# Local transformer: the softmax of the window attention by whole banks of 512 columns

## The chip, the cores and the metric

The program runs on one core of one Trainium2 chip. The metric is the device time of the program in microseconds (us); lower is better. The engines are TensorE (PE; its weight loads are PEld), VectorE (DVE), ScalarE (ACT), GpSimd (POOL) and SyncE (SP), which issues the DMAs.

## The reference, cut to what matters

The program computes two layers of a network on 16 sequences of 256 tokens and 128 features. Its longest part is the local transformer of the first layer: six blocks, each an attention over windows of 32 tokens (16 heads of 64) and a gated FFN. A window's queries see the keys of their own window and of the one before: 64 keys.

```python
q = l2norm(q) * qs
k = l2norm(k) * ksc
...
q = q * cos * scale + rotate_half(q) * sin * scale
k = k * cos * inv + rotate_half(k) * sin * inv
...
sim = jnp.einsum('bhwie,bhwje->bhwij', bq, bk2) * QK_SCALE
sim = jnp.where(mask, -jnp.finfo(sim.dtype).max, sim)
attn = jax.nn.softmax(sim, -1)
out = jnp.einsum('bhwij,bhwje->bhwie', attn, bv2)
```

The norms of `l2norm` are numbers per token and head. The kernel multiplies the inverse norm of a key into the key itself, and that of a query, `rn` (with the scale 8 in the tables), into the softmax.

## The kernel before, in words

The 16 sequences are taken in 8 units of two; a unit's state `z` is 128 features by 512 tokens and stays in SBUF. The local transformer is one loop over `n`, with 32 iterations to a block (8 units x 4), so 192 in all and some to drain. One iteration takes four heads through each stage of a pipeline, and every stage works for another iteration's heads: `n` is projected, `n - 1` rotated, `n - 3` has its key norms fetched, `n - 4` has its keys scaled, its scores and its softmax, `n - 5` has its probabilities transposed, then come the weighted sums (`n - 8`) and the merging into the block's output (`n - 9`). The loop stands under a manual schedule: on PE, DVE, ACT and POOL each engine runs its instructions in the order in which the code writes them. An FFN is a generator whose steps are taken in between (`go_on(behind)`).

Order of one iteration, with the lines of the profile:

1. `scaled` (L837, POOL): keys times their inverse norms, two operations. `merging` (L969, PE): 16 matmuls into the bank `y`.
2. In odd iterations `norms_rows(rk)`: PE transposes `rk` (L816), ACT copies it (L818), SP writes it to DRAM as `rkh`. `widened` (L828, SP) later reads it back into `kn`, spread over partitions.
3. `rotate` (L756, POOL): four additions of what a DMA (`got`) has moved across partitions.
4. `flipped` twice (L930, PE; copies at L938 on ACT and L936 on DVE): the probabilities `pr` are transposed; between the two, `windows` (L847) and `masked` (L863), which fills two score banks with the mask.
5. In even iterations `norms_sum` (L764, PE; L773, ACT). `weighted` (L948, PE; copies L963 on ACT, L961 on DVE).
6. `scores` (L885, PE): 64 small matmuls into the two banks, one for each parity of the heads. Each bank is 8 groups of 64 keys.
7. `maxima` (L897, L899, DVE): for each bank the largest score of each group, then `nb = -mx * rn`.
8. In even iterations `norms_inverse`: PE transposes the sums (L782), DVE clamps them and makes a first guess of the inverse root (L784, L793), POOL refines it in three Newton steps (L800 to L808), 13 small operations. The results are `rk` for the keys (used by step 2 of the next iteration) and `rq`, from which `rn` is cut.
9. `project` twice (L740, PE): query and key of two head pairs, four matmuls in all; ACT squares each bank (L743), DVE makes `sent` and `q` or `k` from it (L745, L748), SP sends `sent` to `got` (L750, L751). `exponentials` is a generator that `project` advances between its banks: 16 exponentials of 64 columns (L907, ACT), each with the bias and the scale of its group and with its sum read out of the accumulator.
10. `divided` (L920, DVE; L922, POOL): reciprocal of 8 sums and the scaling of half of `pr`, done for each half.

PSUM has eight banks: four general ones, used in turn (`mm`), three for scores (`sim`) and one for `y`. `pr` has one buffer.

Of the kernel before, what the change touches and what calls it, by code (L numbers as in the profile page):

```python
# [13 lines left out]
AF = mybir.ActivationFunctionType  # L14
ALU = mybir.AluOpType
# [29 lines left out]
def adaln_kernel(  # L45
# [33 lines left out]
    def small(tag, shape, bufs=4):  # L79
        return (stage.get("small") or sm).tile(list(shape), F32, tag=tag, name=tag, bufs=bufs)  # L80
# [561 lines left out]
    with ExitStack() as es:  # L642
# [133 lines left out]
        def norms_inverse(n2):  # L776


            pt = bank()
            for t in range(4):  # L780
                c = slice(t * 128, (t + 1) * 128)
                nc.tensor.transpose(pt[:, c], n2[:, c], ident)  # L782
            x = small("nx", (128, 4, 4, 4), 2)
            nc.vector.tensor_scalar(  # L784
                x,
                pt.rearrange("p (t g e) -> p t g e", t=4, g=4)[:, :, :, 0:4],
                1e-24,
                None,
                ALU.max,
            )  # L790
            x = x.rearrange("p t g e -> p (t g e)")
            y = small("ny", (128, 64), 2)
            nc.vector.tensor_scalar(  # L793
                y.bitcast(I32), x.bitcast(I32), -0.5, float(0x5F3759DF), ALU.mult, ALU.add
            )
            rk = small("rk", (128, 4, 8), 2)
            rq = small("rq", (128, 8, 4), 3)
            for it in range(3):
                a = small("na", (128, 64), 2)
                nc.gpsimd.tensor_tensor(a, x, y, ALU.mult)  # L800
                nc.gpsimd.tensor_tensor(a, a, y, ALU.mult)
                nc.gpsimd.tensor_scalar(a, a, -0.5, 1.5, ALU.mult, ALU.add)
                if it < 2:
                    nc.gpsimd.tensor_tensor(y, y, a, ALU.mult)
                else:
                    y, a = (v.rearrange("p (t j e) -> p t j e", t=4, j=2) for v in (y, a))
                    nc.gpsimd.tensor_tensor(rk, y[:, :, 0], a[:, :, 0], ALU.mult)
                    nc.gpsimd.tensor_tensor(  # L808
                        rq.rearrange("p e t -> p t e"), y[:, :, 1], a[:, :, 1], ALU.mult
                    )  # L810
            return rk, rq.rearrange("p (g h o) t -> p g h (o t)", g=2, h=2)

        def norms_rows(rk):

# [76 lines left out]
                                skip_group_check=True,  # L891
                            )

        def maxima(sim, rn):

            mx = small("mx", (128, 8))
            nc.vector.tensor_reduce(mx, sim.rearrange("p (b k) -> p b k", b=8), AX.X, ALU.max)  # L897
            nb = small("nb", (128, 8))
            nc.vector.scalar_tensor_tensor(nb, mx, -1.0, rn, ALU.mult, ALU.mult)  # L899
            return nb  # L900

        def exponentials(x, sims, nbs, rn, pr, ssum):

            for par in range(2):
                for st in range(4):
                    b = 4 * x + st
                    nc.scalar.activation(  # L907
                        pr[:, x, st, par, :],
                        sims[par][:, b * 64 : (b + 1) * 64],
                        AF.Exp,  # L910
                        bias=nbs[par][:, b : b + 1],
                        scale=rn[:, par, b : b + 1],
                        accum_out=ssum[:, x, st, par : par + 1],
                    )
                    if st % 2:
                        yield

        def divided(pr, ssum):
            rsum = small("rsum", (128, 8))
            nc.vector.reciprocal(rsum, ssum.rearrange("p t h -> p (t h)"))  # L920
            prf = pr.rearrange("p t h k -> p (t h) k")
            nc.gpsimd.tensor_tensor(  # L922
                prf, prf, rsum.unsqueeze(2).to_broadcast([128, 8, 64]), ALU.mult
            )

        def flipped(p, x, pr, prT):

            pt = bank()
            for st in range(4):
                nc.tensor.transpose(  # L930
                    pt[:, st * 128 : (st + 1) * 128],
                    pr[:, x, st].rearrange("p h k -> p (h k)"),
                    ident,
                )
            if x:
                nc.vector.tensor_copy(prT[:, p + x, :], pt)  # L936
            else:
                nc.scalar.copy(prT[:, p + x, :], pt)  # L938

        def weighted(j, xw, prT):  # L940

# [150 lines left out]
        while n < N + 9 or behind:  # L1092
            layer, at_ = divmod(n, per)
            if at_ == 13 and 0 < layer < DEPTH:
                wffs[layer] = load_ffn(layer)
            if 0 <= n - 4 < N:
                for m in (2 * (n - 4), 2 * (n - 4) + 1):
                    scaled(m, kns.pop(m))

            w, j = divmod(n - 9, QS)  # L1100
            if 0 <= w < DEPTH * NU:
                if j == 0:
                    pys[w] = psy.tile([128, 512], F32, tag="y", name="y")
                merging(j, zxs.pop((w, j)), vos[w // NU], pys[w])
                if j == QS - 1:
                    add_to_state(w % NU, pys.pop(w))
            if n % 2 and 3 <= n <= N + 1:
                home = norms_rows(rk)
            go_on(behind)
            go_on(merges)  # L1110
            if 0 <= n - 1 < N:
                for m in (2 * (n - 1), 2 * (n - 1) + 1):
                    rotate(m, qs[m], got.pop(m))
            if 0 <= n - 5 < N:
                i, u, p = place(n - 5)
                if p == 0:
                    prTs[i, u] = atile("prT", (128, NP, 512))
                flipped(p, 0, prs[n - 5], prTs[i, u])
            for s, lag in ((0, 7), (1, 9)):
                v, r = divmod(n - lag, QS)  # L1120
                if r == 0 and 0 <= v < DEPTH * NU:
                    xws[v, s] = windows(v % NU, s)
            sims = masked() if 0 <= n - 4 < N else None
            if 0 <= n - 5 < N:
                flipped(p, 1, prs.pop(n - 5), prTs[i, u])

            if n % 2 == 0 and 2 <= n <= N:
                n2 = norms_sum([squares.pop(m) for m in range(2 * n - 4, 2 * n)])
            v, r = divmod(n - 8, QS)
            if 0 <= v < DEPTH * NU:  # L1130
                zxs[v, r] = weighted(r, xws[v, r // 2], prTs[v // NU, v % NU])
            go_on(behind)
            if sims:
                m = 2 * (n - 4)
                rn = inverses[m // 4][:, m % 4 // 2]
                scores(sims, m, [qs.pop(m), qs.pop(m + 1)])
                pr = atile("pr", (128, 2, 4, 2, 64), 1)
                nbs = [maxima(sims[par], rn[:, par]) for par in range(2)]
                ssum = small("ssum", (128, 2, 4, 2))

            if n % 2 == 0 and 2 <= n <= N:
                rk, inverses[n // 2 - 1] = norms_inverse(n2)
            if 0 <= w < DEPTH * NU and j == QS - 1:
                behind.append(ffn(w % NU, w // NU))
            go_on(behind)
            between = exponentials(0, sims, nbs, rn, pr, ssum) if sims else iter(())
            for m in (2 * n, 2 * n + 1):
                if n < N:
                    i, u, p = place(n)
                    qs[m], squares[m], got[m] = project(i, u, m, wqk[p + m % 2], between)  # L1150
                if m % 2 == 0:
                    go_on(behind)
            if sims:
                for x in range(2):
                    for _ in between:
                        pass
                    divided(pr[:, x], ssum[:, x])
                    between = exponentials(1, sims, nbs, rn, pr, ssum) if x == 0 else iter(())
                prs[n - 4] = pr
            if 0 <= n - 3 < N:  # L1160
                for m in (2 * (n - 3), 2 * (n - 3) + 1):
                    kns[m] = widened(m, home)
            if layer + 1 < DEPTH:
                if at_ == 18:
                    merges.append(merged(layer + 1))
                if at_ > per - QS:
                    p = 2 * (at_ - (per - QS) - 1)
                    wqk[p : p + 2] = [load_qk(layer + 1, p), load_qk(layer + 1, p + 1)]
            if at_ == 0 and 0 < layer < DEPTH:
                wqk[NP - 2 :] = [load_qk(layer, NP - 2), load_qk(layer, NP - 1)]  # L1170
            n += 1
# [375 lines left out]
```

## Time and profile before

| | us |
|---|---|
| median of 3 runs (4256.94 to 4262.21) | 4258.86 |
| the profiled execution, its own time | 4254.63 |
| its span | 4252.8 |

The busy shares over the span are PE 94%, PEld 61%, DVE 66%, ACT 67%, POOL 62%. The mean granted TensorE clock is 0.983 (1 is full speed). In the page's 40 slices the local transformer fills slices 3 to 33; PE shows 9 (90% or more) in nearly all of them, ACT 6 or 7, and the DMA engines about 4. One iteration takes some 17 us: `scores` starts first at 299.5 us and last at 3572.4.

How to read it: a group of instructions is named by line, engine, operation and tiles (out<-in), with its count; behind the first bar stand its busy time in us and the mean of one in ns, behind the second the idle time of the engine just before it and what ended most of that time. In a timeline a row has its start in us from the span's start, its length, engine, line, operation and tiles, and in brackets the idle time before it. A matmul on float32 operands appears as two records.

### The profile page before, as it was taken

The numbers are of one execution on the slowest core, as the hardware profiler recorded it, in microseconds if no ns is written. First come the engines' busy times: TensorE is split into PE (matmuls) and PEld (weight loads), VectorE is DVE, ScalarE is ACT, GpSimd is POOL, SyncE is SP. The second block draws the span as 40 slices with busy tenths as digits, with TensorE's granted clock in tenths as the row PEclk, the third lists the DMA queues.
The fourth block names the chain that finished last, engine by engine and source line by source line (L and its number), as shares of the span: only waits on it lengthen the run. The fifth ranks groups of instructions, "written<-read, shape, count | busy, mean of one in ns | idle before, by whom it ended". The sixth has DMA issues, their size and how long they took to land.

```text
span 4252.8 us, 118394 instructions
## 1 busy us (share of the span) xinstructions
PE 3979.4 (94%) x45491; PEld 2576.8 (61%) x45491; DVE 2826.8 (66%) x6003; ACT 2839.5 (67%) x9800; POOL 2619.5 (62%) x3326
## 2 busy tenths in 40 slices
PE   7867999999999999999999999999999998899998
PEld 4534666666666666666666666666666666454544
DVE  6746667777676777667676767776676765455554
ACT  4535666766767666666766666766667665578785
POOL 5446666676666776676766677666767673343432
PEclk9889999999999999999999999999999999999999
DMA  1334344444444444444444444444444441100000
GB/s 40 40 95 106 100 108 102 113 103 106 109 100 113 106 108 104 106 115 104 104 107 104 114 101 109 106 105 113 105 104 100 108 102 58 46 3 6 4 6 6
DMA packets 193548, 371.06 MB, mean 87 GB/s; under 512 B 42538, under 2 KB 83417, under 8 KB 192985
## 3 DMA queue, kind: packets, MB, share of 16 engines
q1 hardware_dynamic: 192984, 363.50, 34.2%
q8 instruction: 360, 5.90, 0.6%
q14 instruction: 204, 1.66, 0.1%
HBM read 127.92 MB, written 8.91 MB: 32 GB/s over the span
## 4 chain that ended last, share of the span: by engine, by line
PE 45%; DVE 23%; ACT 19%; issue 6%; POOL 5%; DMA 1%; SPq 0%; POOLq 0%; DVEq 0%; ACTq 0%
ACT pr L907 10%; PE mm L948 9%; PE sim L885 7%; DVE sent L745 6%; PE mm L764 4%; ACT sq L743 4%; PE mm L930 4%; POOL pr L922 4%; DVE k L748 3%; DVE q L748 3%; PE mm L740 3%; DVE mx L897 2%; PE mm L847 2%; PE mm L1334 2%; DVE nb L899 2%
## 5 line engine op out<-in xcount | busy, mean ns | idle before, releaser
L907 ACT ACTIVATE pr<-sim,nb,rq 128x64 f32<-128x64 f32 x3072 | 1229.5, 451 | 336.9 <-DVE nb L899 328.9
L922 POOL TENSOR_TENSOR pr<-pr,rsum 128x512 f32<-128x512 f32 x384 | 398.3, 1042 | 809.9 <-DVE rsum L920 769.4
L907 ACT ACTIVATION_READ_ACCUMULATOR pr<-sim,nb,rq 128x1 f32 x3072 | 773.9, 252 | 0.0
L969 PEld LDWEIGHTS y<-zx,wvo 128*128 128x128 f32 x6144 | 715.7, 192 | 91.5 <-issue 88.7
L969 PE MATMUL y<-zx,wvo 128*128 128x128 f32 x6144 | 717.5, 275 | 1.3 <-ACT zx L963 1.2
L740 PE MATMUL mm<-z,wqk 128*128 128x512 f32 x1536 | 706.4, 602 | 8.6 <-DMA wqk<-in_L_ffn_Wqkv_dram 6.7
L745 DVE SCALAR_TENSOR_TENSOR sent<-mm,vec,rope 128x512 f32<-128x512 f32 x768 | 570.6, 743 | 118.4 <-ACT sq L743 110.2
L756 POOL TENSOR_TENSOR k<-k,got 128x512 f32<-128x512 f32 x384 | 496.1, 1292 | 0.0
L756 POOL TENSOR_TENSOR q<-q,got 128x512 f32<-128x512 f32 x384 | 487.9, 1271 | 12.7 <-DMA got<-sent 10.6
L837 POOL TENSOR_TENSOR k<-k,kn 128x512 f32<-128x512 f32 x384 | 481.8, 1274 | 19.6 <-DMA kn<-rkh 19.6
L743 ACT ACTIVATE sq<-mm 128x512 f32<-128x512 f32 x768 | 475.0, 618 | 24.0 <-PE mm L740 23.9
L740 PEld LDWEIGHTS mm<-z,wqk 128*128 128x128 f32 x1536 | 278.1, 191 | 323.1 <-issue 237.4
L961 DVE COPY zx<-mm 128x512 f32<-128x512 f32 x384 | 265.6, 692 | 256.7 <-PE mm L948 256.7
L963 ACT COPY zx<-mm 128x512 f32<-128x512 f32 x384 | 225.2, 586 | 287.8 <-PE mm L948 287.8
L1307 POOL TENSOR_TENSOR pr<-pr,rsum 128x256 f32<-128x256 f32 (+1 forms) x256 | 206.1, 826 | 317.3 <-DVE rsum L1305 309.9
L948 PE MATMUL mm<-prT,xw 64*128 64x256 f32 x3072 | 389.5, 390 | 3.4 <-DVE zx L961 2.0
L897 DVE TENSOR_REDUCE mx<-sim 128x8 f32<-128x512 f32 x384 | 263.2, 685 | 176.1 <-PE sim L885 176.1
L948 PEld LDWEIGHTS mm<-prT,xw 64*128 64x128 f32 x3072 | 293.5, 187 | 119.8 <-issue 90.4
L930 PE MATMUL mm<-ident,pr 128*128 128x128 f32 x1536 | 246.2, 284 | 106.5 <-POOL pr L922 76.6
L930 PEld LDWEIGHTS mm<-ident,pr 128*128 128x128 f32 x1536 | 175.4, 143 | 272.3 <-POOL pr L922 243.4
L885 PEld LDWEIGHTS sim<-k,q 64*32 64x32 f32 x24576 | 264.9, 105 | 86.7 <-issue 58.4
L885 PE MATMUL sim<-k,q 64*32 64x64 f32 x24576 | 298.8, 226 | 19.1 <-issue 9.8
(250 smaller groups left out, 6545.2 us busy)
## 6 DMA issues: line engine op xcount, KB each, us to landing
got<-sent SPq DMA_DIRECT2D x1536, 128.0 KB
kn<-rkh SPq DMA_DIRECT2D x768, 128.0 KB
xw<-xw SPq DMA_DIRECT2D x96, 256.0 KB
wqk<-in_L_ffn_Wqkv_dram SPq DMA_DIRECT2D x48, 128.0 KB
bhome<-brow SPq DMA_DIRECT2D x1, 3072.0 KB
wv<-in_L_ffn_Wqkv_dram SPq DMA_DIRECT2D x12, 256.0 KB
wo<-in_L_ffn_Wo_dram SPq DMA_DIRECT2D x12, 256.0 KB
xt<-in_x_dram SPq DMA_DIRECT2D x8, 256.0 KB
```

The costliest lines, as they stand in the source:

```text
L740: nc.tensor.matmul(pp, wqk[:, j, :], xs, start=True, stop=True)
L743: nc.scalar.activation(sq, pp, AF.Square)
L745: nc.vector.scalar_tensor_tensor(two(sent[:, j, :]), two(pp), scale, tab[1], ALU.mult, ALU.mult)
L756: nc.gpsimd.tensor_tensor(r, r, two(got[:, j, :]), ALU.add)
L837: nc.gpsimd.tensor_tensor(k, k, two(kn), ALU.mult)
L885: nc.tensor.matmul(sims[par][32 * c : 32 * c + 32, c0 : c0 + 64], q[r, s, t0 : t0 + 32], k[r, s, t0 : t0 + 64], start=False, stop=True, sk ...
L897: nc.vector.tensor_reduce(mx, sim.rearrange("p (b k) -> p b k", b=8), AX.X, ALU.max)
L907: nc.scalar.activation(pr[:, x, st, par, :], sims[par][:, b * 64 : (b + 1) * 64], AF.Exp, bias=nbs[par][:, b : b + 1], scale=rn[:, par, b ...
L922: nc.gpsimd.tensor_tensor(prf, prf, rsum.unsqueeze(2).to_broadcast([128, 8, 64]), ALU.mult)
L930: nc.tensor.transpose(pt[:, st * 128 : (st + 1) * 128], pr[:, x, st].rearrange("p h k -> p (h k)"), ident,)
L948: nc.tensor.matmul(pz[par][:, w * 256 : (w + 1) * 256], xw[r, (2 * k + w) % 8, :], prT[r, :, 64 * k + 32 * w : 64 * k + 32 * w + 32], star ...
L969: nc.tensor.matmul(py[:, j * 128 : (j + 1) * 128], vo[:, h, :], zx[:, h % 2, h // 2, :], start=(h == 0), stop=(h == 2 * NP - 1), skip_grou ...
```

## The change

For each bank VectorE now takes the maximum of each group (`mx`) and subtracts it from the scores, from PSUM into the place of the bank's probabilities in `pr`; GpSimd multiplies that by `rn` in place. ScalarE then takes one plain exponential over each bank's 512 columns, in place, without bias, scale or accumulator. VectorE sums each bank's groups and takes one reciprocal of all 16 sums; GpSimd scales the two halves of `pr` as before, now one after the other.

The generator that `project` advances is `softmaxed`: it yields twice, so its instructions come at the third bank of the iteration, between the first and the second `project` bank pair on ACT and DVE. Both copies of `flipped` are on ACT. `norms_inverse` has become a generator: its first part (transposes, clamp, guess) stays in its place, its Newton steps are emitted after the softmax, at the end of the iteration and before the next one's `scaled`.

```diff
             nc.vector.tensor_scalar(
                 y.bitcast(I32), x.bitcast(I32), -0.5, float(0x5F3759DF), ALU.mult, ALU.add
             )
+            yield
...
-            return rk, rq.rearrange("p (g h o) t -> p g h (o t)", g=2, h=2)
+            yield rk, rq.rearrange("p (g h o) t -> p g h (o t)", g=2, h=2)
...
-        def maxima(sim, rn):
-
+        def bank_of(pr, par):
+
+            return pr[:, :, :, par, :].rearrange("p x s k -> p (x s) k")
+
+        def over_keys(v):
+            return v.unsqueeze(2).to_broadcast([128, 8, 64])
+
+        def logits(sim, rn, dst):
+
+            sim = sim.rearrange("p (b k) -> p b k", b=8)
             mx = small("mx", (128, 8))
-            nc.vector.tensor_reduce(mx, sim.rearrange("p (b k) -> p b k", b=8), AX.X, ALU.max)
-            nb = small("nb", (128, 8))
-            nc.vector.scalar_tensor_tensor(nb, mx, -1.0, rn, ALU.mult, ALU.mult)
-            return nb
-
-        def exponentials(x, sims, nbs, rn, pr, ssum):
-
+            nc.vector.tensor_reduce(mx, sim, AX.X, ALU.max)
+            nc.vector.tensor_tensor(dst, sim, over_keys(mx), ALU.subtract)
+            nc.gpsimd.tensor_tensor(dst, dst, over_keys(rn), ALU.mult)
+
+        def softmaxed(pr):
+
+            yield
+            yield
             for par in range(2):
-                for st in range(4):
-                    b = 4 * x + st
-                    nc.scalar.activation(
-                        pr[:, x, st, par, :],
-                        sims[par][:, b * 64 : (b + 1) * 64],
-                        AF.Exp,
-                        bias=nbs[par][:, b : b + 1],
-                        scale=rn[:, par, b : b + 1],
-                        accum_out=ssum[:, x, st, par : par + 1],
-                    )
-                    if st % 2:
-                        yield
-
-        def divided(pr, ssum):
-            rsum = small("rsum", (128, 8))
-            nc.vector.reciprocal(rsum, ssum.rearrange("p t h -> p (t h)"))
-            prf = pr.rearrange("p t h k -> p (t h) k")
-            nc.gpsimd.tensor_tensor(
-                prf, prf, rsum.unsqueeze(2).to_broadcast([128, 8, 64]), ALU.mult
-            )
+                nc.scalar.activation(bank_of(pr, par), bank_of(pr, par), AF.Exp)
+            ssum = small("ssum", (128, 2, 4, 2))
+            for par in range(2):
+                nc.vector.tensor_reduce(
+                    ssum[:, :, :, par].rearrange("p x s -> p (x s)"), bank_of(pr, par), AX.X, ALU.add
+                )
+            rsum = small("rsum", (128, 16))
+            nc.vector.reciprocal(rsum, ssum.rearrange("p x t h -> p (x t h)"))
+            for x in range(2):
+                prf = pr[:, x].rearrange("p t h k -> p (t h) k")
+                nc.gpsimd.tensor_tensor(
+                    prf, prf, over_keys(rsum[:, 8 * x : 8 * x + 8]), ALU.mult
+                )
+            yield
...
-            if x:
-                nc.vector.tensor_copy(prT[:, p + x, :], pt)
-            else:
-                nc.scalar.copy(prT[:, p + x, :], pt)
+            nc.scalar.copy(prT[:, p + x, :], pt)
...
-                nbs = [maxima(sims[par], rn[:, par]) for par in range(2)]
-                ssum = small("ssum", (128, 2, 4, 2))
+                for par in range(2):
+                    logits(sims[par], rn[:, par], bank_of(pr, par))
 
             if n % 2 == 0 and 2 <= n <= N:
-                rk, inverses[n // 2 - 1] = norms_inverse(n2)
+                newton = norms_inverse(n2)
+                next(newton)
...
-            between = exponentials(0, sims, nbs, rn, pr, ssum) if sims else iter(())
+            between = softmaxed(pr) if sims else iter(())
...
             if sims:
-                for x in range(2):
-                    for _ in between:
-                        pass
-                    divided(pr[:, x], ssum[:, x])
-                    between = exponentials(1, sims, nbs, rn, pr, ssum) if x == 0 else iter(())
+                for _ in between:
+                    pass
                 prs[n - 4] = pr
+            if n % 2 == 0 and 2 <= n <= N:
+                rk, inverses[n // 2 - 1] = next(newton)
```

## The prediction

> **What bounds the kernel now.** I read the page first, then four consecutive iterations of the local transformer (one period of its pattern) as windows, then the timeline of one of them on all engines.
>
> ```profile
> PE 3979.4 (94%) x45491; PEld 2576.8 (61%) x45491; DVE 2826.8 (66%) x6003; ACT 2839.5 (67%) x9800; POOL 2619.5 (62%) x3326
> ...
> L907 ACT ACTIVATE pr<-sim,nb,rq 128x64 f32<-128x64 f32 x3072 | 1229.5, 451 | 336.9 <-DVE nb L899 328.9
> L922 POOL TENSOR_TENSOR pr<-pr,rsum 128x512 f32<-128x512 f32 x384 | 398.3, 1042 | 809.9 <-DVE rsum L920 769.4
> L907 ACT ACTIVATION_READ_ACCUMULATOR pr<-sim,nb,rq 128x1 f32 x3072 | 773.9, 252 | 0.0
> ```
>
> The softmax is ScalarE's largest item, but ScalarE is busy 67% and TensorE 94%. The windows, each from one start of `mx` to the next, give the share inside the stage (columns: window, its length, busy time and instructions of PE, PEld, DVE, ACT, POOL, granted clock, DMA share, GB/s).
>
> ```profile
> 2003.64:2020.46 16.82, 16.54 (x217) 10.60 (x218) 12.78 (x22) 10.60 (x40) 10.38 (x9) 1.00 0.46 114
> 2020.46:2036.58 16.12, 15.34 (x219) 11.94 (x220) 11.56 (x22) 11.03 (x42) 11.63 (x22) 1.00 0.44 101
> 2036.58:2053.85 17.27, 16.99 (x221) 10.45 (x220) 11.18 (x19) 13.60 (x44) 12.86 (x11) 1.00 0.42 106
> 2053.85:2071.42 17.57, 16.79 (x214) 11.25 (x215) 12.78 (x23) 11.90 (x42) 12.37 (x22) 1.00 0.42 101
> ```
>
> Call these A, B, C, D: 67.78 us, of which TensorE is busy 65.66. So TensorE's stream of matmuls sets the pace, at full clock, and all that any change beside it can win is the 2.12 us of gaps (with 47 such periods in 192 iterations, 100 us). B and D, with 22 and 23 instructions on POOL and DVE, hold the Newton steps for the key norms (every second iteration). B, in order of time:
>
> ```profile
> 2020.46 0.69 DVE L897 TENSOR_REDUCE mx<-sim 128x8 f32<-128x512 f32 x1 [0.70 <-PE sim L885]
> ...
> 2023.15 0.32 POOL L800 TENSOR_TENSOR na<-nx,ny 128x64 f32<-128x64 f32 x1 [1.27 <-DVE ny L793]
> ...
> 2027.35 0.26 POOL L807 TENSOR_TENSOR rk<-ny,na 128x32 f32<-128x32 f32 x1
> ...
> 2028.73 0.27 PE L816 MATMUL mm<-ident,rk 128*32 128x128 f32 x1
> ...
> 2029.47 1.04 POOL L922 TENSOR_TENSOR pr<-pr,rsum 128x512 f32<-128x512 f32 x1 [1.66 <-DVE rsum L920]
> ...
> 2030.57 0.66 PE L930 MATMUL mm<-ident,pr 128*128 128x128 f32 x4 [0.78 <-POOL pr L922]
> ```
>
> Newton runs on POOL from 2023.15 to 2027.61, in time that POOL otherwise waits for the exponentials. Its `rk` is transposed on TensorE by L816 1.1 us later, without a wait; `pr` is scaled after that, and TensorE waits 0.78 us for it.
>
> **The change part by part.** Clock zero is the start of the first `mx` of an iteration.
>
> *ScalarE.* Sixteen 64-column exponentials with their accumulator reads go, each pair of them 0.77 us (four records, 2022.02 to 2022.80 in the timeline): 8 x 0.77 = 6.2 us. Two of 512 columns come, at most 0.65 us each (the square L1000, SBUF to SBUF), and one `prT` copy of 0.59 moves over from VectorE: 4.3 us less per iteration. On the path it is worth only what TensorE waits for: nothing beyond the 2.12 above.
>
> *VectorE.* `nb` (0.41 mean) twice, one reciprocal (0.20) and the `prT` copy (0.69) go: 1.7 us. Two subtractions and two sums over 512 columns come. No row shows this subtraction; L997 (PSUM minus SBUF, same size) takes 0.68 and the scalar_tensor_tensors follow each other every 0.66, slowest record 0.75: I take 0.71 from start to start. The sum reads SBUF like L500, 0.685; I take 0.70 (bounds 0.66 and 0.75 for both). That is 2.8 in, 1.1 us more, hidden under TensorE while its banks come free in time. The sum stands between the first and second projection's four operations, so the second projection's banks are freed later; see C.
>
> *GpSimd.* Two scalings by `rn` come, priced as L922 (1.04; upper bound L756, 1.27): 2.1 us on 47.24/4 = 11.8 of 16.9. It fits the sum, but not its place:
>
> *Newton moves.* In the changed program's order POOL does, in an even iteration: two `rn` scalings, two `rsum` scalings, then all thirteen Newton steps, then the next iteration's key scaling. TensorE's order is as before: projection, merging, then the transpose of this very `rk`, and all later matmuls queue behind it (the FFN's, both transposes of `pr`, the weighted sums, the next scores). So the cover of Newton, POOL's wait for the exponentials, is gone, and the transpose waits. For B: four VectorE operations of 0.71 = 2.83; `nx`, `ny` and `fx`, 0.96 from 2022.62 to 2023.58; four operations at 0.66 = 2.64; two sums 1.40; reciprocal 0.20; 0.17 to POOL (2029.30 to 2029.47); two scalings 2.04; Newton 4.46; 0.07 to TensorE: 14.77. (The second `rn` scaling ends at 2.83 + 0.17 + 1.04 = 4.04; behind it ScalarE has at most the FFN's square and the two exponentials, 3 x 0.65, done by 6.0, before the first sum at 6.43: they are not in this chain.) Before, L816 started at 2028.73, that is at 8.27: TensorE stands 6.5 us. From there to the next `mx` it took 7.85, less the 0.78 that `pr` no longer costs, as it is ready at 10.24: B = 14.77 + 7.07 = 21.84.
>
> D has no `fx`: 2.83 + 0.47 + 2.64 + 1.40 + 0.20 + 0.17 + 2.04 + 4.46 + 0.07 = 14.28 against 7.41 (2061.26), a stand of 6.9. The rest was 10.16 with 0.67 of waits before L1041's last matmul and the first transpose: D = 14.28 + 9.49 = 23.77.
>
> C: the FFN's two `fx` operations take 1.48, so the second projection's operations start at 2.83 + 1.48 + 2.64 + 1.40 + 0.20 = 8.55, and free their banks at 9.87 and 11.19. With four banks in turn, the third gate matmul of L1031 takes the first of these and the transpose of `pr` the second: it starts at 11.25 instead of 10.27. C = 17.27 + 0.98 = 18.25 (between 17.3, if the banks come in time, and 19). Newton also delays POOL's key scaling (to 17.4) and rotations (to 24.1) in B, but TensorE's scores start later still, and C's first `rn` scaling is not due before its subtraction. The DMAs of `rkh` and `kn`, behind `rk` on SP's queue, have a whole iteration. A loses only its 0.28 of waiting: 16.54.
>
> *The clock.* Such stands also cost clock. Two answers of this trace, from the start of the stage: windows with the columns above, and one row of TensorE's timeline.
>
> ```profile
> 326.40:329.80 3.40, 1.21 (x3) 0.19 (x1) 3.09 (x6) 3.40 (x15) 1.57 (x2) 1.00 0.03 7
> 329.80:333.30 3.50, 0.00 (x0) 0.00 (x0) 2.75 (x6) 3.50 (x19) 0.58 (x1) 0.51 0.76 173
> 333.30:336.70 3.40, 2.89 (x14) 1.98 (x18) 0.23 (x2) 1.21 (x5) 1.50 (x2) 0.50 0.70 175
> ```
> ```profile
> 333.81 1.11 PE L930 MATMUL mm<-ident,pr 128*128 128x128 f32 x4 [6.21 <-POOL pr L922]
> ```
>
> After TensorE stood 6.21 us the granted clock was 0.50, and four transposes took 1.11 us that take 0.66 at 1.00. Half clock lasted here until 336.7, 2.9 us after work resumed, so 1.45 us were lost; after the stand that ended at 307.2 it lasted until 312.8, so 2.8 were lost. Bounds per stand: 0 (a stand may meet no drop) and 2.8; I take the mean of the two seen, 2.1.
>
> [...]
>
> *Sum.* A 16.54 + B 21.84 + C 18.25 + D 23.77 = 80.40, plus 2 x 2.1 = 84.60, against 67.78: 16.8 per period. Times 47: 790 us (593 from the waits, 197 from the clock). The profiled execution took 4254.6 (span 4252.8), so 5045; the median of the runs lies 4.2 above it: 5050.
>
> **The rivals.** *Clock stays up.* The waits as above, no drop: 5050 - 197 = 4853; for it, `rk`'s wait might be split by stray matmuls; against it, no matmul stands between merging and L816 to do so.
>
> *Longer still.* Half clock for 2.8 us of loss per stand (66 us more) and every VectorE operation at its upper bound (six of them on the chain, 0.3 per stand, 28 us): 5145. For it: POOL and VectorE are both fuller.
>
> *Faster.* The transpose of `rk` is not late, and what is left is the gain: B 0.78, D 0.67, A 0.28, against C's 0.98 if the banks do bind: at best -1.7 x 47 = -81, so 4178. It decides once Newton ends by 8.2 (B) and 7.3 (D), so starts by 3.7 and 2.8; but POOL's order puts it behind `pr`, which needs the sums, and even with exponentials and sums run at once after the second `rn` scaling (ends at about 4) it can't begin before 8.
>
> *Nothing.* ScalarE's relief is hidden, and Newton too: 4259. The same argument speaks against it.
>
> **How the numbers follow.** The forecast 5050 gets 0.60, clock up 0.19, longer 0.18, faster 0.025, nothing 0.005. Range: from 4825 (clock up at 4853, and C's banks late by little more than a third of 0.98, 28 less) to 5170 (longer, with C at 18.8). What a measurement here can tell from no change is about 0.2%, 9 us: faster 0.025, same 0.005, slower 0.97.
>
> **What would show it.** In the profile after: TensorE idle some 6.5 us before the transpose of `rk` 96 times, released by POOL's `rk`, some 600 us in all; granted clock near 0.9 in the stage, dipping to half after each stand; POOL's Newton behind the `pr` scalings; ScalarE's busy time down by some 800 us (192 x 4.3); no wait of the `pr` transposes on POOL in B and D. Wrong if the transpose starts without a wait, if the clock stays at 1.00, or if C, not B and D, grows.

## The result, and the profile after

| | before | after |
|---|---|---|
| median, us | 4258.35 (4 runs, 4256.94 to 4262.21) | 5047.78 (4 runs, 5046.13 to 5048.91) |
| profiled execution, us | 4254.63 | 5046.13 |
| span, us | 4252.8 | 5044.3 |
| granted clock | 0.983 | 0.894 |
| TensorE busy, us | 3979.4 | 4234.6 |
| TensorE not busy (span less busy), us | 273.4 | 809.7 |

The changed kernel takes 1.185 times as long (95% interval 1.183 to 1.187). The last two rows split the loss: 45491 matmul records stand in both profiles, and they take 255 us longer, which is clock (experiment 3 tests it); TensorE stands 536 us longer, which is waiting. Together that is the 791.5 us by which the span grew.

The busy line and two groups of the page after (busy us and mean ns, then the idle time before and what ended it):

```profile
PE 4234.6 (84%) x45491; PEld 2737.1 (54%) x45491; DVE 3110.5 (62%) x6003; ACT 2039.4 (40%) x4232; POOL 3002.4 (60%) x3710
...
L925 POOL TENSOR_TENSOR pr<-pr,rsum 128x512 f32<-128x512 f32 x384 | 392.5, 1044 | 796.5 <-DVE rsum L922 796.5
...
L817 PE MATMUL mm<-ident,rk 128*32 128x128 f32 x96 | 37.7, 393 | 632.5 <-POOL rk L808 632.5
```

ScalarE's two costliest groups are gone and its busy time fell by 800 us, yet the kernel is slower: that engine was not the bound. One small matmul, L817 (L816 before), now ends 632.5 us of TensorE's idle time in 96 places, 6.6 us each. Its releaser is the Newton step that makes `rk`, L808, on POOL. In the kernel before, the same wait stood at (us in all, times, longest us):

```profile
PE mm L816 <- POOL rk L807: 11.7, 4, 4.5
```

Four consecutive iterations as windows, from one first `mx` to the next; in the prediction's names they are B, C, D, A (columns as there):

```profile
2347.39:2372.85 25.46, 18.95 (x218) 13.97 (x219) 13.38 (x22) 7.01 (x13) 17.15 (x26) 0.80 0.30 72
2372.85:2390.26 17.41, 17.09 (x221) 10.68 (x222) 12.18 (x19) 9.48 (x15) 10.99 (x10) 1.00 0.38 92
2390.26:2416.43 26.17, 19.13 (x214) 12.55 (x214) 14.87 (x23) 7.67 (x13) 15.77 (x24) 0.80 0.26 63
2416.43:2432.72 16.29, 16.29 (x217) 10.54 (x218) 13.59 (x21) 6.36 (x11) 11.32 (x10) 1.00 0.46 118
```

The whole loss lies in B and D, the iterations with Newton steps (26 and 24 POOL instructions): about 6.5 and 7.0 us in which TensorE is not busy, and a clock of 0.80. C and A (17.41 and 16.29) are within 0.6 us of what they were. D in order of time, from the timeline of all engines:

```profile
2390.26 0.69 DVE L906 TENSOR_REDUCE mx<-sim 128x8 f32<-128x512 f32 x1 [0.67 <-PE sim L886]
...
2393.15 1.04 POOL L908 TENSOR_TENSOR pr<-pr,rq 128x512 f32<-128x512 f32 x1 [0.22 <-DVE pr L907]
2393.24 1.01 DVE L793 TENSOR_SCALAR ny<-nx 128x64 int32<-128x64 int32 x1
...
2396.80 1.26 DVE L918 TENSOR_REDUCE ssum<-pr 128x8 f32<-128x512 f32 x2
...
2398.49 2.04 POOL L925 TENSOR_TENSOR pr<-pr,rsum 128x512 f32<-128x512 f32 x2 [4.30 <-DVE rsum L922]
2400.49 0.32 POOL L801 TENSOR_TENSOR na<-nx,ny 128x64 f32<-128x64 f32 x1
...
2404.69 0.25 POOL L808 TENSOR_TENSOR rk<-ny,na 128x32 f32<-128x32 f32 x1
...
2405.00 0.39 PE L817 MATMUL mm<-ident,rk 128*32 128x128 f32 x1 [7.04 <-POOL rk L808]
```

POOL stands 4.30 us waiting for the sums, scales both halves of `pr`, and only then runs Newton, for which `nx` and `ny` have been ready since 2394.25. The time in which Newton used to run is still there (the 4.30 us), but it lies ahead of it in POOL's order. The clock in the same place, in windows of 3.41 us:

```profile
2400.00:2403.41 3.41, 0.00 (x0) 0.00 (x0) 1.03 (x2) 0.00 (x0) 2.83 (x9) 0.60 0.51 115
2403.41:2406.82 3.41, 1.82 (x3) 0.91 (x4) 0.00 (x0) 0.26 (x1) 3.08 (x8) 0.50 0.17 38
2406.82:2410.24 3.42, 3.42 (x5) 1.10 (x4) 1.50 (x2) 0.00 (x0) 3.42 (x4) 0.50 0.02 5
2410.24:2413.65 3.41, 3.41 (x26) 2.86 (x26) 1.43 (x2) 1.65 (x3) 2.26 (x2) 0.90 0.02 5
```

Work is back at 2405.0, but the clock is half until about 2410.9 (the last window's mean is 0.90, so 0.2 of it was at half speed). That is 5.9 us of work at half speed.

### The profile page after: what moved, and what is told of

It is laid out like the page before. It is cut to its first block, busy times and chain, and to the rows that moved or that the text cites. A ratio compares the mean times of both kernels' runs of the same rounds, so it can differ in the third digit from the quotient of the medians.

```text
span 5044.3 us, 113537 instructions
## 1 busy us (share of the span) xinstructions
PE 4234.6 (84%) x45491; PEld 2737.1 (54%) x45491; DVE 3110.5 (62%) x6003; ACT 2039.4 (40%) x4232; POOL 3002.4 (60%) x3710
## 4 chain that ended last, share of the span: by engine, by line
PE 57%; DVE 21%; POOL 12%; issue 6%; ACT 3%; DMA 1%; SPq 0%; DVEq 0%; POOLq 0%; ACTq 0%
PE mm L949 7%; PE y L970 6%; PE sim L886 6%; PE mm L1042 5%; PE mm L934 4%; PE mm L740 4%; POOL pr L925 4%; DVE pr L907 4%; DVE mx L906 4%; PE mm L764 3%; DVE sent L745 3%; PE mm L1032 2%; PE mm L848 2%; DVE ssum L918 2%; PE mm L1055 2%
## 5 line engine op out<-in xcount | busy, mean ns | idle before, releaser
L740 PE MATMUL mm<-z,wqk 128*128 128x512 f32 x1536 | 736.5, 612 | 44.7 <-DVE fx L998 22.9
L908 POOL TENSOR_TENSOR pr<-pr,rq 128x512 f32<-128x512 f32 x384 | 400.4, 1044 | 545.9 <-DVE pr L907 544.6
L743 ACT ACTIVATE sq<-mm 128x512 f32<-128x512 f32 x768 | 434.5, 590 | 535.1 <-PE mm L740 532.7
L817 PE MATMUL mm<-ident,rk 128*32 128x128 f32 x96 | 37.7, 393 | 632.5 <-POOL rk L808 632.5
L939 ACT COPY prT<-mm 128x512 f32<-128x512 f32 x384 | 224.6, 585 | 702.6 <-PE mm L934 696.0
L756 POOL TENSOR_TENSOR q<-q,got 128x512 f32<-128x512 f32 x384 | 488.3, 1272 | 23.2 <-DMA got<-sent 20.1
L756 POOL TENSOR_TENSOR k<-k,got 128x512 f32<-128x512 f32 x384 | 488.9, 1273 | 0.0
L740 PEld LDWEIGHTS mm<-z,wqk 128*128 128x128 f32 x1536 | 267.2, 191 | 400.1 <-issue 182.9
L949 PE MATMUL mm<-prT,xw 64*128 64x256 f32 x3072 | 401.6, 402 | 0.7 <-ACT prT L939 0.7
L817 PEld LDWEIGHTS mm<-ident,rk 128*32 128x32 f32 x96 | 9.8, 102 | 652.6 <-POOL rk L808 652.6
L819 ACT COPY rkT<-mm 32x128 f32<-32x128 f32 x96 | 24.5, 256 | 824.3 <-PE mm L817 824.3
L1046 DVE SCALAR_TENSOR_TENSOR fg<-mm,vec,fg 128x512 f32<-128x512 f32 x144 | 107.7, 749 | 370.9 <-PE mm L1042 370.1
L934 PEld LDWEIGHTS mm<-ident,pr 128*128 128x128 f32 x1536 | 237.4, 173 | 165.1 <-issue 116.8
```

The lines of the kernel that those rows point to most:

```text
L740: nc.tensor.matmul(pp, wqk[:, j, :], xs, start=True, stop=True)
L743: nc.scalar.activation(sq, pp, AF.Square)
L756: nc.gpsimd.tensor_tensor(r, r, two(got[:, j, :]), ALU.add)
L908: nc.gpsimd.tensor_tensor(dst, dst, over_keys(rn), ALU.mult)
L934: nc.tensor.transpose(pt[:, st * 128 : (st + 1) * 128], pr[:, x, st].rearrange("p h k -> p (h k)"), ident,)
L949: nc.tensor.matmul(pz[par][:, w * 256 : (w + 1) * 256], xw[r, (2 * k + w) % 8, :], prT[r, :, 64 * k + 32 * w : 64 * k + 32 * w + 32], star ...
```

## The experiments

The theory: the loss is the place of the Newton steps on POOL, which delays the transpose of `rk` and with it all of TensorE, and the clock that such stands cost. The first rival: the new softmax itself (two more scalings on GpSimd and, in sum, 1.1 us more on VectorE per iteration) makes the kernel slower. The second, on the size: waits alone, no clock. Diffs are against the changed kernel unless another is named. Medians are given beside those of the kernel before in the same batch of runs (4252 to 4260); 2 to 4 ran twice each, the others four times or more.

**1. Newton back in its old place, the new softmax kept.**

```diff
                 newton = norms_inverse(n2)
                 next(newton)
+                rk, inverses[n // 2 - 1] = next(newton)
...
-            if n % 2 == 0 and 2 <= n <= N:
-                rk, inverses[n // 2 - 1] = next(newton)
```

> The new softmax kept whole, the Newton steps emitted at their old place, right behind the first guess (on GpSimd behind the scalings by rn, ahead of those by rsum). Theory (the place of Newton makes the loss): the transpose of rk waits 0.3 us in B and 1.2 us in D instead of 6.0 and 7.0, the clock stays at 1.00, a period comes back to about 67.7 us, total 4255 us (4220 to 4300). Rival (the new softmax itself, with fuller VectorE and GpSimd, makes the loss): above 4600 us.

Measured 4264.1, ratio 1.002 (1.001 to 1.003). The busy line of its page and its row of waits (idle us in all, times, longest us; so in all rows of waits below):

```profile
PE 3969.3 (93%) x45491; PEld 2571.1 (60%) x45491; DVE 3109.0 (73%) x6003; ACT 2038.5 (48%) x4232; POOL 3009.0 (71%) x3710
```
```profile
PE mm L817 <- POOL rk L808: 55.3, 51, 5.0
```

One line moved, and 784 us are back. ScalarE is as little busy as in the changed kernel, VectorE and GpSimd as much, and the time is that of before within 0.3%. So the new softmax brings nothing, 801 us off an engine that does not set the pace, and costs about 10 us, 0.2%.

**2. The old softmax, with only the Newton steps moved** (against the kernel before; `norms_inverse` is a generator as in the change).

```diff
-                rk, inverses[n // 2 - 1] = norms_inverse(n2)
+                newton = norms_inverse(n2)
+                next(newton)
...
+            if n % 2 == 0 and 2 <= n <= N:
+                rk, inverses[n // 2 - 1] = next(newton)
```

> The old softmax kept whole, only the Newton steps moved behind the scalings of pr. Theory: the old pr is ready later (11.7 us after the first mx in B, 12.4 in D, against 10.2 and 9.7 predicted for the new one), so rk comes at 16.2 and 16.9 and TensorE stands 8 to 9.5 us: about 5220 us (5100 to 5350), slower than with both parts. Rival (the new softmax makes the loss): about 4260 us.

Measured 5146.2, ratio 1.209 (1.206 to 1.211).

```profile
PE mm L817 <- POOL rk L808: 793.3, 96, 11.2
```

The move alone is worse than the whole change: the stands are 8.3 us each (793.3 / 96) against 6.6. In an iteration like B (first `mx` at 2316.74) POOL's last scaling of `pr` ends 11.7 us after the first `mx`, against 10.9 in the changed kernel, and TensorE is through with its work ahead of the transpose 8.4 us after it, against 9.3. With 1, the rival of the new softmax falls. Where Newton stands last, the new softmax is even 98 us better than the old one; where Newton stands in its old place, it is 0.2% slower.

**3. Added matmuls in the stand**: seven matmuls of 128x512 into a score bank that is overwritten unread, ahead of each transpose of `rk`.

```diff
             if n % 2 and 3 <= n <= N + 1:
+                fill = pss.tile([128, 512], F32, tag="sim", name="fill")
+                for _ in range(7):
+                    nc.tensor.matmul(
+                        fill, ident, rope[:, 0].rearrange("p a t -> p (a t)"), start=True, stop=True
+                    )
                 home = norms_rows(rk)
```

> The changed kernel with seven added 128x512 matmuls, read by nobody, on TensorE right ahead of each transpose of rk: 7 x 0.86 = 6.0 us of work that fills the stand. Theory (about 255 us of the loss is clock lost after the stand): granted clock back to 0.98, the time falls by about 250 us to about 4800 us (4760 to 4850), although work was added. Rival (matmuls after the stand are slow for another reason, or the clock is granted by something else): 5048 us or more.

Measured 4795.7, ratio 1.126 (1.124 to 1.129): work was added, and 252 us went. The granted clock is 0.986. TensorE's timeline around one stand:

```profile
2317.77 6.17 PE L1111 MATMUL fill<-rope,ident 128*128 128x512 f32 x14
2323.92 0.28 PE L817 MATMUL mm<-ident,rk 128*32 128x128 f32 x1
2324.04 1.00 PE L1005 MATMUL mm<-mean,fs 128*128 128x1 f32 x8
```

The filler takes 6.17 us at full clock, and here the transposition follows without a wait; in 48 of the 96 places it still waits, 56.4 us in all. Behind the stand in the changed kernel's B, the same eight records of L1005 take 1.75 us:

```profile
2362.73 0.40 PE L817 MATMUL mm<-ident,rk 128*32 128x128 f32 x1 [6.00 <-POOL rk L808]
2362.91 1.75 PE L1005 MATMUL mm<-mean,fs 128*128 128x1 f32 x8
```

This separates the two costs, roughly. The fillers are busy 592.7 us in all; without them TensorE is busy 289 us less than in the changed kernel (4538.1 - 592.7 against 4234.6), and the fillers and the standing left (254.6) take 37 us more than its 809.7 of standing. So the drops of the clock cost 250 to 290 us, where the split of the busy time said 255, and the 542 us left over the kernel before are in the main the stands themselves (536 by the split).

**4. The transpose moved behind the scores**, Newton left last.

```diff
-            if n % 2 and 3 <= n <= N + 1:
-                home = norms_rows(rk)
             go_on(behind)
...
                     logits(sims[par], rn[:, par], bank_of(pr, par))
+            if n % 2 and 3 <= n <= N + 1:
+                home = norms_rows(rk)
```

> The changed kernel with the transpose of rk moved on TensorE from ahead of the FFN steps to behind the scores. Newton stays behind the scalings of pr. If the transpose's wait were all that Newton's place costs: about 4180 us. Theory: GpSimd's queue is late next; the key scaling behind Newton ends at 17.9 us in B and 17.4 in D, the scores of the following iteration wait for it, and the rotations behind it make C's scaling by rn late: a period of about 72 us, total about 4450 us (4370 to 4530), clock near 0.98.

Measured 4503.3, ratio 1.058 (1.056 to 1.060); the transpose waits no more, but POOL's key scaling does:

```profile
POOL k L838 <- DMA kn<-rkh: 259.2, 55, 8.8
```

The norms now come late over SP: the transfers of `kn` stand in another place of SP's queue. The time is in the expected range, but the expectation had reckoned with GpSimd's own queue and not with SP's, and the run does not part the two. It shows only that 544 of the 789 us go when the transpose stands elsewhere, with Newton still last.

**5. Newton back (as in 1), the transpose behind both `flipped`.** After 1, what was left to win were the last waits on `rk`.

```diff
-            if n % 2 and 3 <= n <= N + 1:
-                home = norms_rows(rk)
...
                 flipped(p, 1, prs.pop(n - 5), prTs[i, u])
+            if n % 2 and 3 <= n <= N + 1:
+                home = norms_rows(rk)
```

> The first experiment (Newton at its old place, new softmax kept) with the transpose of rk moved on TensorE behind the two transposes of pr. The first experiment's TensorE still waited 55 us in all for rk (0.87 us in D). Theory: that wait goes, since rk is ready before the first transpose of pr is over, and nothing else is late: about 4215 us (4195 to 4240). Rival (TensorE only waits for pr there instead): 4264 us.

Measured 4321.9, ratio 1.016 (1.0145 to 1.0175): a miss. The wait on `rk` went, and one on `kn` of the size of that in 4 came (242.5 us in 51 places). SP's own timeline, and POOL's next row:

```profile
2014.96 1.75 SPq L829 DMA_DIRECT2D kn<-rkh  x3
...
2026.79 0.60 SPq L751 DMA_DIRECT2D got<-sent  x1
2027.43 5.71 SPq L829 DMA_DIRECT2D kn<-rkh  x5
```
```profile
2030.74 1.28 POOL L838 TENSOR_TENSOR k<-k,kn 128x512 f32<-128x512 f32 x1 [4.43 <-DMA kn<-rkh]
```

SP's order is not written by hand here. With the transpose emitted later, the eight loads of `kn` are here split 3 and 5 around the eight `got` transfers, no longer 4 and 4 (the next pair of iterations has 4 and 4 again), and the fourth load, which POOL's key scaling needs, waits behind all `got`.

**6 to 8, and 10. More work moved ahead of the scores**, to cover the wait for the maximum: in 6 the FFN's step and the first guess (`nx`, `ny`) on top of 5; in 7 the same three moves on the kernel before; in 8 without moving the transpose, so that SP's order is the old one; in 10 the moves of 8 on the kernel before. The core of all four:

```diff
             go_on(behind)
+            if 0 <= w < DEPTH * NU and j == QS - 1:
+                behind.append(ffn(w % NU, w // NU))
+            go_on(behind)
+            if n % 2 == 0 and 2 <= n <= N:
+                newton = norms_inverse(n2)
+                next(newton)
             if sims:
                 m = 2 * (n - 4)
```

> The same, and two pieces of VectorE's work moved ahead of the scores: the FFN's step (fx, 0.7 to 1.5 us in B and C) and the first guess of the norms (nx, ny, 1.2 us in B and D). In the first experiment TensorE waited 0.51 us in B and 0.38 in C for fx, and 0.59 in C for the bank that q leaves. [...] Rival (what waits is only pushed to the next bank): 4215 us or more.

> The kernel before, old softmax, with the same three moves (rk's transpose behind those of pr; the FFN's step and the first guess ahead of the scores). If the new softmax is worth something once Newton is out of the way, this stays above the run before it: pr still ends with ScalarE's sixteen exponentials and TensorE still waits 0.8 us for it in B and 0.5 in D, so about 4225 us (4200 to 4250). Rival (the moves alone make the gain, the softmax is worth nothing): about 4160 us.

> As the run with all three moves, but rk's transpose at its old place ahead of the FFN steps, so that SyncE's queue keeps its old order (rkh, xw, four loads of kn; in the run with all moves one or two of a pair's four loads stood behind the next iteration's eight got). Theory (that order made the three misses): GpSimd's wait for kn falls from 269 us to some 20, TensorE's waits for fx in B and C and for q's bank in C go, its 0.9 us for rk in D stays: about 4190 us (4160 to 4225). Rival (the VectorE work put ahead of the scores makes the loss): above 4300 us.

> The kernel before, old softmax, with the same two pieces of VectorE's work ahead of the scores and nothing else. Theory: pr still ends with ScalarE's sixteen exponentials, so only the 0.6 us that TensorE waited for fx in C go, and a little of pr's wait: about 4225 us (4200 to 4250), above the new softmax with the same moves. Rival (the moves alone make the gain): within 0.3% of that run.

Measured 4430.9, 4443.7, 4406.1 and 4424.7 (ratios 1.042, 1.045, 1.035 and 1.040, each within 0.002): four misses, 6 against some 4160 forecast. In 8 the wait for `kn`, 268.5 us in 6, is nearly gone, but that for `rk` is 145.6 where 1 had 55.3:

```profile
PE mm L817 <- POOL rk L808: 145.6, 95, 5.2
POOL k L838 <- DMA kn<-rkh: 52.5, 12, 6.7
```

So SP's queue is not the main cause in these four; the moves themselves cost. By the pages, 8 has 65.5 us more standing than 1 and 85.6 more busy time (clock). In 10 neither of the two waits is large (`rk` 7.6 us, `kn` 18.7). There TensorE waits for what the moved FFN makes (52.3 us for `fg`, 40.2 for `fs`, about 2 for each in the kernel before) and longer for `pr` (99.9 against 76.6), and its busy time is 60.5 longer; no run tests this further. Old and new softmax under the same moves differ by 0.4% (8 against 10) and 0.3% (6 against 7), here with the new one ahead, where 1 had it 0.2% behind: by itself it is worth next to nothing. Why work ahead of the scores costs some 140 us in 8 (against 1) was followed up by 9 alone.

**9. Only the FFN's step ahead of the scores, Newton back.** The diff is that of 8 without the first guess.

> The first experiment with only the FFN's step moved ahead of the scores; the norms' first guess stays behind the two subtractions. Theory: 0.51 us in B and 0.97 in C go, 70 us in all, about 4195 us. If the first guess ahead matters, the other run is clearly below this one; if only the FFN's step does, they agree within 0.3%.

Measured 4339.3, ratio 1.019 (1.017 to 1.021): a miss, and 75 us worse than 1. 8, with the first guess ahead as well, is slower by 67 us more, so each of the two moves costs. The two profiled spans differ by 86.4 us, of which 61.6 are busy time (clock) and 24.8 standing, by the two pages. The waits of `rk` doubled (112.5 us in 96 places against 55.3 in 51); the likely reason is that the FFN's matmuls had covered a part of Newton from behind the scores. One of the stands, as windows and in TensorE's timeline:

```profile
1957.79:1961.20 3.41, 2.45 (x20) 1.93 (x18) 3.36 (x7) 0.64 (x2) 3.16 (x8) 1.00 0.59 135
1961.20:1964.60 3.40, 3.16 (x13) 2.18 (x14) 0.68 (x1) 1.01 (x3) 3.34 (x4) 0.50 0.70 159
```
```profile
1958.91 0.28 PE L817 MATMUL mm<-ident,rk 128*32 128x128 f32 x1 [0.87 <-POOL rk L808]
1959.03 1.00 PE L1005 MATMUL mm<-mean,fs 128*128 128x1 f32 x8
```

The stand is 0.87 us and TensorE is busy 2.45 of the 3.41 us before the drop, and still the next window runs at 0.50. A part of the 2.45 are the eight one-column records of L1005, which count 1.00 us here; no run removed them, so whether they have a part in the drop is not shown.

**11. The first guess ahead of the subtractions**, Newton left last. `logits` yields behind the first maximum and at its end, and `norms_inverse`'s first part is emitted between:

```diff
             nc.vector.tensor_reduce(mx, sim, AX.X, ALU.max)
+            yield
             nc.vector.tensor_tensor(dst, sim, over_keys(mx), ALU.subtract)
```

> The changed kernel with the norms' first guess (nx, ny) put on VectorE between the first maximum and the first subtraction, where GpSimd has no scaling by rn under way; nothing else moved. In the changed kernel ny takes 1.01 us beside GpSimd's scaling, 0.20 in the kernel before. [...] Rival (the longer record is covered by something else on the chain): 5048 us.

Measured 4911.9, ratio 1.154 (1.152 to 1.156): 136 us better than the changed kernel; about 4970 was forecast. The rows of L793 (count, then shortest, median and longest ns), in the changed kernel and in this one:

```profile
L793 DVE TENSOR_SCALAR ny<-nx x96: 787/1006/1148, 286.2 to 4319.9; 128x64 int32<-128x64 int32 x96
```
```profile
L793 DVE TENSOR_SCALAR ny<-nx x96: 194/196/1315, 283.8 to 4183.3; 128x64 int32<-128x64 int32 x96
```

The median of `ny` is 1.01 us in the changed kernel, where 95 of the 96 overlap a scaling by `rn` on GpSimd and the last a rotation, and 0.20 here, ahead of those scalings. Some 0.8 us on the chain, 96 times, is 78 us; the idle time fell by 63, of which 42 are the wait for `rk` (632.5 to 590.1). The gain is larger than forecast because the clock gave 73 more (busy time 4234.6 to 4161.3, granted clock 0.894 to 0.911). In the clock records of both traces the spells at half speed last whole windows of 3.41 us (in the changed kernel 111 of 112): 90 of 112 spells last three windows in the changed kernel, and 66 of 111 only two in this one.

**12. What the runs suggest: Newton back, the first guess early, the transpose one FFN step later**, as far as SP's order stays the old one. The diffs of 1 and 11, and

```diff
-            if n % 2 and 3 <= n <= N + 1:
-                home = norms_rows(rk)
             go_on(behind)
             go_on(merges)
+            if n % 2 and 3 <= n <= N + 1:
+                home = norms_rows(rk)
```

> The first experiment (Newton at its old place) with the first guess early as in the other run and rk's transpose one FFN step later on TensorE, still ahead of the rotations, so that SyncE's queue keeps its order. Theory: fx is ready 0.35 us earlier in B, and in D about half of the 0.87 us for rk goes, the rest becoming a wait for k's bank: about 4225 us (4200 to 4250), the first below the kernel before. Rival (as in the earlier misses, a shorter wait only comes back elsewhere): 4255 us or more.

Measured 4216.4 (4211.5 to 4219.0), ratio 0.9895 (0.988 to 0.991): 1% faster than the kernel before, and the only one here that is. Its row of waits for the transpose:

```profile
PE mm L817 <- POOL rk L808: 18.5, 7, 5.5
```

Against 1, TensorE stands 259.0 us instead of 289.6, and the waits on `rk` have fallen from 55.3 to 18.5. Which of the two moves brought how much wasn't tried apart.

## Why the prediction was right

*What bounds, and ScalarE.* Right. ScalarE's busy time fell by 800 us, 4.2 per iteration for 4.3 forecast, and experiment 1 shows that this is worth nothing.

*The chain to `rk`.* Right in kind, and nearly in size: 14.77 us after the first `mx` forecast in B, 15.34 measured (2362.73, from TensorE's timeline, less 2347.39); 14.28 and 14.74 in D (2405.00 less 2390.26). The term that was too small is "`nx`, `ny`": 0.47 us from the trace of before became 1.17 (2392.99 to 2394.16), because `ny` ran beside the new `rn` scaling (1.01 us for 0.20; experiment 11). The trace of before could have warned: its longest `ny` is 1.09 us at a median of 0.20, and the three of its 96 that take over 1 us are the only ones that overlap a GpSimd operation (a rotation, L756). In D `ny` starts at 2393.24, and GpSimd's scaling runs from 2393.15 to 2394.19; why `ny` is longer beside it, no run shows. The other terms were a little too large: the two sums took 1.30 (2396.80 to 2398.10) for 1.40, the four operations for maxima and differences 2.73 for 2.83.

*The stands.* 6.5 and 6.9 us forecast; 6.00 and 7.04 in the two iterations shown, 6.6 in the mean of 96. In B two errors cancel: the chain was 0.57 longer than forecast, and TensorE came to the transpose 9.34 us after the first `mx` and not at 8.27, where the sum had left it.

*C's banks.* Wrong. C was to grow by 0.98 us, since the second projection frees its banks later; it took 17.41 for 18.25 forecast (17.27 before). The gate matmuls and the transposes of `pr` did start later in C, the transposes 10.73 us after the first `mx` (2383.58) instead of 10.27, but for 11.25 forecast, and 0.32 of that came back before the next `mx`. The lower bound given for C, 17.3, was the right value.

*The sum of the waits.* 593 forecast, 536 measured. Without C's 0.98 the forecast would have been 547 (593 less 47 x 0.98): C is most of the difference. The small gains beside it are as forecast: the wait of `pr`'s transposes on POOL fell from 76.6 to 13.2 us.

*The clock.* Right in kind, too small: 2.1 us per stand forecast from two samples, 255.2 / 96 = 2.66 measured. The rows of D above show when the clock changes: a mean of 0.60 in the window from 2400.00 puts the fall at 2400.68, and 0.90 in that from 2410.24 puts the return at 2410.92, 10.24 us later, three times 3.41. The same grid, continued back, fits B, whose clock returns at 2369.96, nine times 3.41 ahead of the fall in D. Windows cut on this grid, three of B and then two of D:

```profile
2363.13:2366.55 3.42, 3.42 (x18) 3.20 (x18) 0.16 (x1) 0.88 (x3) 3.36 (x4) 0.50 0.02 5
2366.55:2369.96 3.41, 3.41 (x15) 2.32 (x14) 0.68 (x1) 1.12 (x2) 3.41 (x4) 0.50 0.24 53
2369.96:2373.37 3.41, 3.41 (x147) 2.88 (x144) 1.90 (x3) 1.17 (x2) 1.94 (x2) 1.00 0.64 180
...
2404.09:2407.50 3.41, 2.50 (x4) 1.25 (x5) 0.32 (x1) 0.26 (x1) 3.24 (x6) 0.50 0.02 5
2407.50:2410.92 3.42, 3.42 (x7) 1.33 (x6) 1.51 (x3) 0.00 (x0) 3.42 (x4) 0.50 0.00 0
```

In D the window in which the stand ends, 2.50 of 3.41 us busy, was followed by another at 0.50; behind that one, busy throughout, the clock was back at 1.00, and 5.9 us of work ran at half speed. In B the window from 2363.13 is busy throughout by the records, with most of the eight one-column records of L1005 in it, and was still followed by another at 0.50, so 7.2 us of work ran at half speed (2362.73 to 2369.96). In the prediction's first sample, by contrast, the clock was back behind a window with 2.89 of 3.40 us busy, and 1.45 us were lost. So the price behind a stand differs from stand to stand, and two samples could not give its mean; whether it goes with where the stand ends in the grid or with what runs behind it, no run shows. By the busy time it is 2.66 us here, 2.0 behind the longer stands of experiment 2 ((4171.6 - 3979.4) / 96) and 1.9 in experiment 11.

*The total.* 5050 forecast, 5047.8 measured. The closeness is partly luck: waits too large by 57 us and clock too small by 58 cancel. Of the rivals, "clock stays up" (4853) fails on the granted clock of 0.894; experiment 3 is what it would have looked like, at 4795.7. "Longer still" had the loss of clock nearly right (2.8 per stand) and a longer chain, but for a wrong reason: the VectorE operations stayed below its upper bounds, and what grew was `ny`.

## What to carry to other kernels

When an edit moves a producer on an engine that runs in order, look for its consumer on the engine that sets the pace, and count what the producer now stands behind: here thirteen tiny operations, moved behind a wait, cost 20.9% by themselves and 18.5% together with the large rewrite, which by itself costs 0.2%. Relief for an engine that isn't the bound should be booked at zero, and a stand of TensorE at its own length plus the clock behind it, here 2.7 us for each stand of 6.6 (2.0 for each of 8.3 in experiment 2). A matmul moved in the code can move the DMAs that follow it in a queue whose order the builder chooses: read that queue's timeline after each such move.

## What the runs showed of the hardware that was not expected

- Added matmuls made the kernel faster: seven per stand, 96 times, with a gain of 252 us, as the clock stayed at 0.986 instead of 0.894.
- A VectorE `tensor_scalar` of 128x64 took 1.01 us instead of 0.20 beside a GpSimd operation of 1.04 us.
- The clock fell to 0.50 behind a window in which TensorE was busy 2.45 of 3.41 us by its records and stood 0.87, with eight one-column records in it (experiment 9), and in B of the changed kernel it stayed at 0.50 behind a window busy 3.42 of 3.42 us with most of such a group in it. What decides the clock there stays open.
